# A perceiver block on one core: the last 65 context rows of each batch, taken as one half-length section per four batches

## The chip, the cores and the metric

The kernel runs on one core of one Trainium2 chip. Its time is the device time of one execution in microseconds (us); of a kernel that was run several times the median is given. The profile is taken from one further execution, which has a time of its own. The engines have short names here: PE is TensorE (PEld its weight loads), DVE is VectorE, ACT is ScalarE, POOL is GpSimd, SP is SyncE, which here issues DMAs. A name with a q (SPq) is the instruction queue of that engine.

## The reference, cut to what matters

Everything is float32. Eight batches of 64 rows of 512 numbers go through three blocks with residual sums: a cross attention to a context of 1601 rows per batch, a causal attention among the 64 rows, and a mixture of eight experts with two shared ones. The change lies in the cross attention:

```python
k = key_value @ Wk.T + bk          # key_value: (8, 1601, 512), Wk: (512, 512)
v = key_value @ Wv.T + bv
scores = einsum('bhqd,bhkd->bhqk', q, k) / sqrt(32)      # 16 heads of 32
s = where(scores >= 0, scores + 1, 1 / (1 - scores))
attn = s / sum(s, -1)
context = einsum('bhqk,bhkd->bhqd', attn, v)             # then @ Wo.T + bo
```

So 8 x 1601 context rows are multiplied by two 512 x 512 matrices, and each product is used by one batch.

## The kernel before, in words

**Sections and products of halves.** The 1601 rows of a batch are three sections of 512 rows and a rest of 65 (`TAIL`), of which the 64 that begin the rest are called `ROUND`. For a section the product with a weight matrix is not taken as eight products of half-size blocks but as seven, by sums and differences of blocks (Strassen's scheme in Winograd's form). `weight_parts` (L323) forms four sums of blocks of a weight matrix on DVE, `right_parts` and `context_part` (L334, L341) four differences of blocks of the section on POOL, `multiply` (L353) one of the seven products on PE, and `products` (L365) hands out the seven as units: each is copied out of PSUM by ACT, joined by DVE, and in one case added on POOL. The list `ORDER` says which bank of PSUM each product adds to: the units 0, 2, 4, 6 share bank A, 3 and 5 share B, 1 has C. `products(i, True)` gives the keys of section i, `products(i, False)` its values. The seven units of a whole section and one matrix take `7 * PROD` of planned time, with `PROD = FULL / 2 = 1.715`.

**The rest of a batch.** `load_tail(b)` (L472), `tail_keys(b)` (L482) and `tail_values(b)` (L502) treat the 65 last rows of two batches, b and b + 1, together, and without products of halves: 16 matmuls of 130 columns for the keys, 4 of 512 columns for the values. They are called for b = 0, 2, 4, 6. The value of the very last row (row 1600) of all batches is formed once at the start by `plain_values(odd_x, odd_v, B)` (L444), and a small DMA that POOL issues puts it under the other 64 values of its batch (L512).

**The plan.** `Plan` holds units of PE work with planned lengths, `plan.add`, and other work that is due at a planned time, `plan.at`. `emit` writes all of it out in the order of these times. Attention is spread evenly over it: `step = (end - 14.0) / len(tiles_in)` is the planned time of a tile of 128 context rows, with `end` the planned end of all sections; `lag` sets the first tile behind the sections that it needs. A unit of attention (two tiles, or the one rest of a batch) has `score` on PE (four PSUM banks), four times `convert` (three ACT instructions, a reciprocal on DVE of 128x512 and an addition and sums on POOL), and `weigh` on PE (L622). Within an engine, the compiler's scheduler takes the instructions that it thinks ready, in the order of the text; after `act.bind()`, at the end of the first section's part, ACT keeps the order of the text exactly.

**Memory.** PSUM has 7 banks of the pool `ps_a` and one for the output of attention. In SBUF the pool `w8` has 14 buffers of 8 KB per partition: `wk`, `wv` and their sums (`sk`, `sv`) stay in four of them, the others go round among a section's rows (`cx`), its differences (`tx`), keys, values and the weights of the later blocks. The pool `at` has 5 buffers for the converted scores, and `tl` holds what belongs to the rests.

**Before the first section.** SP loads the first section, then the four tiles of x (`res`), the rests of batches 0 and 1 (`cxt`), and the second section; the ACT queue loads `wk`, `wv`, `wq`. PE multiplies section 0 with `wk` chunk by chunk as both arrive (`first_keys`, four PSUM banks that ACT copies out), then come `plain_values`, `tail_keys(0)`, `tail_values(0)`, the four layer norms of x (`first_rows`), the first two units of the values of section 0, the queries, and the rest of these values. The sums `sq` of `wq` are formed at the very start; `sv` and `sk` during the queries, by `sums_of_weights`.

Of the kernel before, what the change touches and what calls it, by code (L numbers as in the profile page):

```python
# [18 lines left out]
P = 128  # L19
# [18 lines left out]
SEC = 512  # L38
# [57 lines left out]
def perceiver_kernel(  # L96
# [78 lines left out]


# [21 lines left out]
    bk_t = bias_cols(bk, NC, "bk_t")  # L198
    wv = load_w(wvT, "wv", nc.scalar)
# [72 lines left out]
    class Norm:  # L272
# [11 lines left out]
        def factors(self):  # L284
            self.rs = lnp.tile([P, 1], F32, name="ln_rs")
            act.activation(self.rs, self.mv[:, 1:2], AF.Sqrt, bias=eps_t)
            nc.vector.reciprocal(self.rs, self.rs)
            self.nb = lnp.tile([P, 1], F32, name="ln_nb")
            nc.vector.scalar_tensor_tensor(
                self.nb, self.mv[:, 0:1], -1.0, self.rs, ALU.mult, ALU.mult  # L290
            )
# [31 lines left out]
    def weight_parts(w, name):  # L323
        parts = {"a11": w[:, 0:2, 0:256], "a12": w[:, 2:4, 0:256],
                 "a21": w[:, 0:2, 256:512], "a22": w[:, 2:4, 256:512]}
        t = w8(name).rearrange("p k (c f) -> p k c f", c=2)
        for k in range(4):
            parts[f"s{k + 1}"] = t[:, k]
        for d, a, b, op in (("s1", "a21", "a22", ALU.add), ("s2", "s1", "a11", ALU.subtract),
                            ("s3", "a11", "a21", ALU.subtract), ("s4", "a12", "s2", ALU.subtract)):  # L330
            nc.vector.tensor_tensor(parts[d], parts[a], parts[b], op)
        return parts

    def right_parts(x, n=SEC):  # L334
        return {"b11": x[:, 0:2, 0 : n // 2], "b12": x[:, 0:2, n // 2 : n],
                "b21": x[:, 2:4, 0 : n // 2], "b22": x[:, 2:4, n // 2 : n]}

    RIGHT = (("t1", "b12", "b11"), ("t2", "b22", "t1"), ("t3", "b22", "b12"), ("t4", "b21", "t2"))
    tparts = {}
# [25 lines left out]
    def products(i, keys, w=None, dst=None, scale=None, bias=bk_t):  # L365
# [27 lines left out]
        def unit(n):  # L393
            bank, a, b = ORDER[n]
            if n == 0:
                t = dst
                if t is None:
                    t = (kTs if keys else vs)[i] = w8("kT" if keys else "v")
                for f in range(2):
                    for r in range(2):  # L400
                        st[f, r] = t[:, 2 * f : 2 * f + 2, r * HF : (r + 1) * HF] if keys else \
                            t[:, 2 * r : 2 * r + 2, f * 256 : (f + 1) * 256]
            fresh = bank not in st
            if fresh:
                st[bank] = psa("ps_k" if keys else "ps_v").rearrange("p (k n) -> p k n", k=2)
            ps = st[bank]
            multiply(ps, w[a], tparts[i][b], keys, first=fresh)
            if n == 0:
                copy(st[0, 0], ps, 0)
            elif n == 1:  # L410
                join(st[0, 0], ps)
            elif n == 2:
                copy(st[0, 1], ps, 0)
            elif n == 3:
                copy(st[1, 1], ps, None)
            elif n == 4:
                u3 = snp.tile([P, 2, 256], F32, tag="sn", name="u3")
                copy(u3, ps, 1)
                nc.gpsimd.tensor_add(st[1, 1], st[1, 1], u3)
            elif n == 5:  # L420
                join(st[0, 1], ps)
            else:
                copy(st[1, 0], ps, 1)
# [26 lines left out]

    tails = {}

    ROUND = TAIL - 1


    odd_x = const.tile([P, NC, B], F32, name="odd_x")
    for c in range(NC):
        nc.gpsimd.dma_start(
            out=odd_x[:, c, :],
            in_=ctxT[:, c * P : (c + 1) * P, SKV - 1 : SKV].rearrange("b p s -> p (b s)"),  # L460
        )
    odd_v = const.tile([B, E], F32, name="odd_v")
# [7 lines left out]


    def load_tail(b):  # L472

        cx = tails[b, "x"] = tlp.tile([P, NC, 2 * TAIL], F32, name="cxt", bufs=1)
        for k in range(2):
            nc.sync.dma_start(
                out=cx[:, :, k * ROUND : (k + 1) * ROUND],
                in_=ctxT[b + k, :, NSEC * SEC : SKV - 1].rearrange("(c p) s -> p c s", p=P),
            )
        nc.gpsimd.tensor_copy(cx[:, :, 2 * ROUND :], odd_x[:, :, b : b + 2])  # L480

    def tail_keys(b):  # L482
        kT = tlp.tile([P, NG, 2, TAIL], F32, name="kTt")
        cx = tails[b, "x"]
        for g in range(NG):
            ps = psa("ps_kt")[:, : 2 * TAIL]
            for c in range(NC):
                nc.tensor.matmul(  # L488
                    ps, wk[:, c, g * P : (g + 1) * P], cx[:, c, :], start=c == 0, stop=c == NC - 1
                )  # L490
            for s in (slice(0, ROUND), slice(ROUND, TAIL)):
                act.activation(
                    kT[:, g, :, s],
                    ps[:, 2 * s.start : 2 * s.stop].rearrange("p (k s) -> p k s", k=2),
                    AF.Identity, bias=bk_t[:, g : g + 1],
                )
        for k in range(2):
            tails[b + k, "k"] = kT[:, :, k, :]

    def tail_values(b):  # L502
        x = tails[b, "x"]
        ps = psa("ps_vt")
        for c in range(NC):
            nc.tensor.matmul(  # L506
                ps, x[:, c, 0 : 2 * ROUND], wv[:, c, :], start=c == 0, stop=c == NC - 1
            )
        for k in range(2):
            v = tails[b + k, "v"] = tlp.tile([P, E], F32, name="vt")  # L510
            act.copy(v[:ROUND], ps[k * ROUND : (k + 1) * ROUND])
            nc.gpsimd.dma_start(out=v[ROUND:TAIL, :], in_=odd_v[b + k : b + k + 1, :])  # L512
# [11 lines left out]
    def first_rows(tt):  # L524
# [4 lines left out]
        norm.stats()  # L529
# [535 lines left out]
    for i, (b, k) in enumerate(secs):  # L1065
        if i == 0:
# [3 lines left out]
            plan.at(0.05, lambda: (load_tail(0), weigh_bq(), wqp.update(weight_parts(wq, "sq"))))  # L1070
            plan.add(FULL, lambda: plain_values(odd_x, odd_v, B))
            plan.add(FULL, lambda: tail_keys(0))
            plan.add(FULL, lambda: tail_values(0))
            for tt in range(NTT):
                plan.add(0.5, lambda tt=tt: first_rows(tt))
            for n in range(4):
                plan.at(plan.now + 0.01 * n, lambda n=n: context_part("q", n))
            def sums_of_weights(to, w, name):

                with tc.issue_after(products.join.ins):  # L1080
                    to.update(weight_parts(w, name))

            plan.at(plan.now + 3.5 * PROD, lambda: sums_of_weights(wvp, wv, "sv"))
            plan.at(plan.now + 7.5 * PROD, lambda: sums_of_weights(wkp, wk, "sk"))
            wvp.update({"a11": wv[:, 0:2, 0:256], "a12": wv[:, 2:4, 0:256]})
# [32 lines left out]
        if k == NSEC - 1:  # L1118
            if b % 2 == 0 and b:
                plan.at(plan.now - 20.0, lambda b=b: load_tail(b))  # L1120
                plan.add(FULL, lambda b=b: tail_keys(b))
                plan.add(FULL, lambda b=b: tail_values(b))
# [22 lines left out]
    for u, time in enumerate(when):  # L1145
# [4 lines left out]
        if u == 3 * nu:  # L1150
            plan.at(time, clear)
    for tt in range(NTT):
# [578 lines left out]
```

## Time and profile before

| | us |
|---|---|
| median of 3 runs | 1362.18 (1360.87 to 1362.47) |
| the profiled execution | 1363.89 |
| its span, first to last instruction | 1362.3 |
| PE busy | 1349.4 (99%) |
| DVE busy | 977.8 (72%) |
| ACT busy | 676.2 (50%) |
| POOL busy | 765.1 (56%) |

A page of the profile gives the busy time of the engines, the span in 40 slices, the chain of work that ended last, and groups of equal instructions (count, busy time, mean time of one, idle time of the engine ahead of them and what ended it). Further views show the same trace in order of time, in stretches, or by tile. In the order-of-time view a row has the start, the time that the merged instructions took together, engine, line of the kernel, operation, output and inputs, shape and count. Each float32 matmul leaves two records, so a count of 8 is four matmuls. A record's own time holds the time that it needs to run through the array; what a record costs PE in a stream is the distance to the next start. The context is sent to SBUF with its rows as columns, so "128x130" is 130 context rows.

### The profile page before, as it was taken

Reading aid. Unit: us, or ns where it says so; the run is one execution under the profiler, and the core shown is the slowest. Engines: PE = TensorE matmul, PEld = TensorE weight load, DVE = VectorE, ACT = ScalarE, POOL = GpSimd, SP = SyncE. Lnnn points to the kernel's source line nnn. Section 1 sums busy time; section 2 is a strip of 40 time slices with the busy share of each in tenths; the row PEclk is TensorE's granted clock in tenths of the full one; section 3 lists DMA queues with packets and bytes.
Section 4 is the critical chain, followed back from the end, with each engine's and each line's share of the span. In section 5 each row is a group of like instructions: output and inputs, shape, how many; then the busy total and the mean of one; then the engine's idle time right before and its main releaser. Section 6 shows DMA issues by size and latency. Waiting matters only on the chain.

```text
span 1362.3 us, 37675 instructions
## 1 busy us (share of the span) xinstructions
PE 1349.4 (99%) x16554; PEld 1118.1 (82%) x16554; DVE 977.8 (72%) x859; ACT 676.2 (50%) x1436; POOL 765.1 (56%) x682
## 2 busy tenths in 40 slices
PE   9999999999999999999999999999999999999997
PEld 6888888888788888878888877578898999977786
DVE  2899999997999997999998999876976300010314
ACT  3566666665766666666656667435322211122230
POOL 3999999887978887888878876710200000000020
PEclk9999999999999999999999999999999999999999
DMA  7111111122401131112122104256555937788731
GB/s 210 64 33 33 33 33 64 33 79 72 156 10 64 33 110 41 33 33 63 42 62 81 64 33 163 88 177 238 190 200 157 337 133 266 265 303 322 274 92 32
DMA packets 87212, 160.63 MB, mean 118 GB/s; under 512 B 13467, under 2 KB 15035, under 8 KB 87045
## 3 DMA queue, kind: packets, MB, share of 16 engines
q1 hardware_dynamic: 79988, 140.61, 30.5%
q0 software_dynamic: 4704, 13.91, 2.9%
q10 hardware_dynamic: 2352, 3.67, 0.9%
q8 instruction: 131, 2.15, 0.7%
q14 instruction: 37, 0.30, 0.1%
HBM read 147.44 MB, written 10.72 MB: 116 GB/s over the span
## 4 chain that ended last, share of the span: by engine, by line
PE 95%; DMA 2%; DVE 1%; ACT 1%; issue 0%; SPq 0%; DVEq 0%
PE ps_v L359 22%; PE ps_k L359 21%; PE ps_h L1564 9%; PE ps_hh L359 7%; PE ps_hr L359 7%; PE ps_s L572 6%; PE y L1476 4%; PE y L1485 4%; PE ps_o L622 4%; PE y L1052 2%; PE ps_h L1040 2%; PE ps_aq L729 1%; PE ps_kt L488 1%; PE ps_vt L506 1%; PE ps_ap L801 1%; PE ps_wo L679 1%
## 5 line engine op out<-in xcount | busy, mean ns | idle before, releaser
L590 DVE RECIPROCAL neg<-neg 128x512 f32<-128x512 f32 (+1 forms) x224 | 686.9, 3096 | 55.0 <-ACT neg L87 48.5
L591 POOL TENSOR_TENSOR at<-at,neg 128x512 f32<-128x512 f32 (+1 forms) x224 | 269.3, 1208 | 107.5 <-DVE neg L590 100.1
L603 POOL TENSOR_TENSOR tot<-tot,at 128x512 f32<-128x512 f32 (+1 forms) x176 | 223.7, 1271 | 13.3
L87 ACT ACTIVATE neg<-neg,one_t 128x512 f32<-128x512 f32 (+1 forms) x224 | 157.8, 705 | 0.0
L87 ACT ACTIVATE neg<-ps_s 128x512 f32<-128x512 f32 (+1 forms) x224 | 127.9, 571 | 55.4 <-PE ps_s L572 54.8
L1564 PEld LDWEIGHTS ps_h<-xgT,w1t 128*128 128x128 f32 x896 | 123.0, 191 | 27.8 <-issue 26.1
L1569 ACT ACTIVATE hT<-ps_h,b1e 128x128 f32<-128x128 f32 (+3 forms) x112 | 42.6, 380 | 194.9 <-PE ps_h L1564 194.9
L359 PE MATMUL ps_v<-sv,tx 128*128 128x256 f32 x576 | 134.3, 383 | 0.0
L1564 PE MATMUL ps_h<-xgT,w1t 128*128 128x128 f32 (+3 forms) x896 | 129.2, 287 | 0.0
L1467 POOL DMA_DIRECT2D ys_d<-yo x10 | 5.4, 541 | 219.6 <-DVE yo L1466 219.6
L87 ACT ACTIVATE at<-ps_s 128x512 f32<-128x512 f32 (+1 forms) x224 | 128.5, 574 | 0.0
L359 PE MATMUL ps_k<-tx,sk 128*128 128x256 f32 x552 | 128.4, 384 | 0.0
L359 PEld LDWEIGHTS ps_v<-sv,tx 128*128 128x128 f32 x576 | 107.2, 190 | 17.0 <-issue 1.9
L359 PEld LDWEIGHTS ps_k<-tx,sk 128*128 128x128 f32 x552 | 102.7, 190 | 16.0 <-ACT at L87 0.8
L87 ACT COPY v<-ps_v 128x512 f32<-128x512 f32 x96 | 56.4, 588 | 93.7 <-PE ps_v L359 93.6
L87 ACT ACTIVATE kT<-ps_k,bk_t 128x256 f32<-128x256 f32 (+1 forms) x142 | 60.3, 478 | 66.9 <-PE ps_k L359 66.9
L1458 DVE COPY xgT<-pt_x 128x512 f32<-128x512 f32 (+3 forms) x12 | 6.8, 593 | 119.4 <-PE pt_x L1457 119.4
L359 PE MATMUL ps_v<-wv,cx 128*128 128x256 f32 x384 | 89.7, 383 | 0.6 <-DVE kT L387 0.6
L359 PE MATMUL ps_k<-cx,wk 128*128 128x256 f32 x368 | 86.2, 384 | 2.0 <-ACT at L87 1.3
L572 PEld LDWEIGHTS ps_s<-qT,kT 32*64 32x64 f32 x6144 | 70.3, 130 | 17.0 <-issue 14.5
L359 PEld LDWEIGHTS ps_v<-wv,cx 128*128 128x128 f32 x384 | 71.6, 190 | 12.3 <-DVE kT L387 1.5
L359 PEld LDWEIGHTS ps_k<-cx,wk 128*128 128x128 f32 x368 | 68.6, 190 | 12.3 <-ACT at L87 1.5
(286 smaller groups left out, 2258.8 us busy)
## 6 DMA issues: line engine op xcount, KB each, us to landing
w1t<-in_W_dram SPq DMA_DIRECT2D x32, 1024.0 KB, 10.4
w2t<-in_W_dram SPq DMA_DIRECT2D x32, 1024.0 KB, 9.7
cx<-in_ctxT_dram SPq DMA_DIRECT2D x23, 1024.0 KB, 5.2
w1t<-in_sW_dram SPq DMA_DIRECT2D x14, 1024.0 KB, 6.5
w2t<-in_sW_dram SPq DMA_DIRECT2D x14, 1024.0 KB, 6.0
wo<-in_woT_dram SPq DMA_DIRECT2D x4, 1024.0 KB, 5.5
awq<-in_aWq_dram SPq DMA_DIRECT2D x4, 1024.0 KB, 5.6
awp<-in_aWp_dram SPq DMA_DIRECT2D x4, 1024.0 KB, 5.6
```

The source lines that it names most:

```text
L87: ins = getattr(self.engine, name)(*args, **kw)
L359: nc.tensor.matmul(ps[:, k, :], l[:, c, k * P : (k + 1) * P], r[:, c, :], start=first and k == 0 and c == 0, stop=last and c == 1, skip_gr ...
L572: nc.tensor.matmul(ps[j][h, k, g, :], kT[rows, g, h], qT[rows, g, b * SQ : (b + 1) * SQ], start=True, stop=True, skip_group_check=True,)
L590: nc.vector.reciprocal(neg, neg)
L591: nc.gpsimd.tensor_add(pos, pos, neg)
L603: nc.gpsimd.tensor_add(tot, tot, at[:, :, i])
L622: nc.tensor.matmul(accs[b][32 * j : 32 * j + 32, g, :], v[:w, (4 * g + j) * 32 : (4 * g + j + 1) * 32], at[j // 2][:w, j % 2, k, g, :], st ...
L1040: nc.tensor.matmul(ps[:, :N0], w0[0, q][:, c, r * P : (r + 1) * P], shared_x["x"][:, c, :N0], start=c == 0, stop=c == NC - 1,)
L1476: nc.tensor.matmul(self.y[k], hT[:, s : s + w], w2t, start=first, stop=last)
L1485: nc.tensor.matmul(y[d // 2][:, d % 2, :], w2t[:, d * P : (d + 1) * P], hT[:, : self.n], start=first and d % 2 == 0, stop=last, skip_group ...
L1564: nc.tensor.matmul(ph[:, : blk.n], w1t[:, c, f : f + P], blk.x[:, c, :], start=c == 0, stop=c == NC - 1,)
L1569: nc.scalar.activation(hT[:, : blk.n], ph[:, : blk.n], AF.Gelu, bias=blk.bias(hc))
```

## The change

The rests of four batches, without their last rows, are 4 x 64 = 256 rows: half the length of a section. They are now loaded together (`load_tails`, for h = 0 and h = 1), into a `w8` buffer whose other half takes the four differences (`tail_parts`, POOL), and multiplied as seven products of halves with the same block sums of the weights (`tail_products`), keys and values. `products` has gained a half length `hf`. The first four batches are done at the start, the other four after the last section of batch 4. The values go to a DRAM tile `vt_d`, from which SP reads 65 rows for each batch (`load_vt`). The last rows of all batches are padded to 32 columns and multiplied with `wk` and `wv` in four strips of 32 output partitions (`odd_rows`); four transposes turn their keys. The sums `sk` and `sv` are now formed at the very start, the layer norms' statistics are put behind them on DVE, and `sq` behind the layer norms. The loads of the first rests stand ahead of those of x on SP.

```diff
+    ROUND = TAIL - 1
+    NQB = B // 2
+
+    def load_tails(h):
+        t = w8("cxt")
+        cxs["t", h] = t[:, :, 0:256]
+        for k in range(NQB):
+            nc.sync.dma_start(
+                out=t[:, :, k * ROUND : (k + 1) * ROUND],
+                in_=ctxT[h * NQB + k, :, NSEC * SEC : SKV - 1].rearrange("(c p) s -> p c s", p=P),
+            )
+        tparts["t", h] = right_parts(t, 256) | {
+            f"t{n + 1}": t[:, n, 256:512].rearrange("p (c s) -> p c s", c=2) for n in range(4)
+        }
...
     bk_t = bias_cols(bk, NC, "bk_t")
+    tparts = {}
+    load_tails(0)
     wv = load_w(wvT, "wv", nc.scalar)
...
-    def products(i, keys, w=None, dst=None, scale=None, bias=bk_t):
+    def products(i, keys, w=None, dst=None, scale=None, bias=bk_t, hf=HF, fit=lambda ps: ps):
...
-                st[bank] = psa("ps_k" if keys else "ps_v").rearrange("p (k n) -> p k n", k=2)
+                st[bank] = psa("ps_k" if keys else "ps_v")[:, : 2 * hf].rearrange(
+                    "p (k n) -> p k n", n=hf if keys else 256
+                )
             ps = st[bank]
             multiply(ps, w[a], tparts[i][b], keys, first=fresh)
+            ps = fit(ps)
...
-    odd_v = const.tile([B, E], F32, name="odd_v")
+    odd_k = const.tile([P, NG, B], F32, name="odd_k")
+    vt_d = dram.tile([B, TAIL, E], F32, name="vt_d")
...
-    def load_tail(b):
-    def tail_keys(b):
-    def tail_values(b):
...
+    def odd_rows():
+        ps = psa("ps_odd")
+        for c in range(NC):
+            for j in range(4):
+                w = (wk, wv)[j // 2]
+                nc.tensor.matmul(
+                    ps[32 * j : 32 * j + 32, 0:256], odd_x[:, c, :],
+                    w[:, c, (j % 2) * 256 : (j % 2 + 1) * 256],
+                    start=c == 0, stop=c == NC - 1, skip_group_check=True,
+                )
+        rows = [np2("odd") for _ in range(2)]
+        for j in range(4):
+            act.copy(
+                rows[j // 2][0:B, (j % 2) * 256 : (j % 2 + 1) * 256], ps[32 * j : 32 * j + B, 0:256]
+            )
+        nc.scalar.dma_start(
+            out=vt_d[:, ROUND:TAIL, :].rearrange("b o e -> b (o e)"), in_=rows[1][0:B, :]
+        )
+        pt = psa("pt_odd")[:, : NG * B].rearrange("p (g b) -> p g b", g=NG)
         for g in range(NG):
+            nc.tensor.transpose(pt[:, g, :], rows[0][0:B, g * P : (g + 1) * P], ident[0:B, 0:B])
+        for g in range(NG):
+            act.activation(odd_k[:, g, :], pt[:, g, :], AF.Identity, bias=bk_t[:, g : g + 1])
+
+    def tail_parts(h):
+        p = tparts["t", h]
+        for d, a, b in RIGHT:
+            nc.gpsimd.tensor_tensor(p[d], p[a], p[b], ALU.subtract)
+
+    def tail_products(h):
...
+        def values():
+            v = tails["v", h] = at4("vh").rearrange("p (k e) -> p k e", k=2)
+            return v
+        ku = products(
+            ("t", h), True, dst=keys, hf=P,
+            fit=lambda ps: ps.rearrange("p k (b s) -> p k b s", s=ROUND),
+        )
+        vu = products(("t", h), False, dst=values, hf=P)
...
+            for k in range(NQB):
+                nc.sync.dma_start(
+                    out=vt_d[h * NQB + k, 0:ROUND, :],
+                    in_=v[(k % 2) * ROUND : (k % 2 + 1) * ROUND, k // 2, :],
                 )
+        return ku[:2] + vu[:2] + ku[2:] + vu[2:-1] + [last]
+
+    def load_vt(b):
+        tails[b, "v"] = tlp.tile([P, E], F32, name="vt")
+        nc.sync.dma_start(out=tails[b, "v"][0:TAIL, :], in_=vt_d[b])
...
-            plan.at(0.05, lambda: (load_tail(0), weigh_bq(), wqp.update(weight_parts(wq, "sq"))))
-            plan.add(FULL, lambda: plain_values(odd_x, odd_v, B))
-            plan.add(FULL, lambda: tail_keys(0))
-            plan.add(FULL, lambda: tail_values(0))
+            def early():
+                tail_parts(0)
+                wkp.update(weight_parts(wk, "sk"))
+                wvp.update(weight_parts(wv, "sv"))
+                early.done = weight_parts.last
+                weigh_bq()
+            def sums_q():
+                with tc.issue_after(Norm.last.ins):
+                    wqp.update(weight_parts(wq, "sq"))
+            plan.at(0.05, early)
+            plan.add(2.0, odd_rows)
+            for u in tail_products(0):
+                plan.add(PROD / 2, u)
             for tt in range(NTT):
-                plan.add(0.5, lambda tt=tt: first_rows(tt))
+                plan.add(0.5, lambda tt=tt: first_rows(tt, early.done))
+            plan.at(plan.now, sums_q)
...
-            plan.at(plan.now + 3.5 * PROD, lambda: sums_of_weights(wvp, wv, "sv"))
-            plan.at(plan.now + 7.5 * PROD, lambda: sums_of_weights(wkp, wk, "sk"))
...
-            if b % 2 == 0 and b:
-                plan.at(plan.now - 20.0, lambda b=b: load_tail(b))
-                plan.add(FULL, lambda b=b: tail_keys(b))
-                plan.add(FULL, lambda b=b: tail_values(b))
+            if b == NQB:
+                plan.at(plan.now - 30.0, lambda: load_tails(1))
+                plan.at(plan.now - 15.0, lambda: tail_parts(1))
+                for u in tail_products(1):
+                    plan.add(PROD / 2, u)
...
+        if units[u][1] == nu - 1:
+            plan.at(time, lambda b=units[u][0]: load_vt(b))
```

In `first_rows` the statistics now carry `tc.issue_after(behind.ins)`: an order on DVE, not a wait for data.

## The prediction

> **What bounds the kernel now.** I read the page first: the busy time of the engines, then the chain of work that ended last.
>
> ```profile
> PE 1349.4 (99%) x16554; PEld 1118.1 (82%) x16554; DVE 977.8 (72%) x859; ACT 676.2 (50%) x1436; POOL 765.1 (56%) x682
> PE 95%; DMA 2%; DVE 1%; ACT 1%; issue 0%; SPq 0%; DVEq 0%
> ```
>
> PE is busy from end to end and is nearly the whole chain; so the change is worth what it takes from PE's stream, less the time in which it makes PE wait. Second, the view in order of time, PE alone, at the two kinds of place where rests are done: the start, and (from the view of all engines) the rest of batches 4 and 5.
>
> ```profile
> 19.99 3.59 PE L447 MATMUL ps_v<-wv,odd_x 128*8 128x512 f32 x8
> 23.99 3.82 PE L488 MATMUL ps_kt<-cxt,wk 128*128 128x130 f32 x32 [0.41 <-DMA cxt<-in_ctxT_dram]
> 27.64 3.60 PE L506 MATMUL ps_vt<-wv,cxt 128*128 128x512 f32 x8
> 31.08 1.91 PE L302 MATMUL pt<-ident,xn 128*128 128x128 f32 x16
> ```
>
> ```profile
> 519.24 3.85 PE L488 MATMUL ps_kt<-cxt,wk 128*128 128x130 f32 x32
> 522.92 3.60 PE L506 MATMUL ps_vt<-wv,cxt 128*128 128x512 f32 x8
> 526.45 3.95 PE L729 MATMUL ps_aq<-xnT_a,awq 128*64 128x64 f32 x128
> ```
>
> Look at the starts: 11.09 us from 19.99 to 31.08, and 7.21 us from 519.24 to 526.45. The other two rests read the same way: 3.67 + 3.63 us at 308 to 319, 3.68 + 3.64 us at 728 to 738.
>
> **Removed from PE.** 11.09 + 7.30 + 7.21 + 7.32 = 32.9 us, including 0.4 us of waiting for `cxt`.
>
> **Added to PE.** Three shapes, each with a row of this trace. Products of halves with 128 columns exist already in the shared expert; with 256 columns in every section; four strips of 32 outputs in the sums of attention:
>
> ```profile
> 896.31 3.73 PE L359 MATMUL ps_hh<-xnT,w1t 128*128 128x128 f32 x32
> 899.88 1.95 PE L359 MATMUL ps_hh<-xt,sw 128*128 128x128 f32 x16
> ```
>
> ```profile
> 99.22 1.89 PE L359 MATMUL ps_k<-cx,sk 128*128 128x256 f32 x8
> 100.94 1.89 PE L359 MATMUL ps_k<-tx,wk 128*128 128x256 f32 x8
> ```
>
> ```profile
> 153.69 0.64 PE L643 MATMUL ps_sum<-tot,ones 128*32 128x256 f32 x8
> 154.26 1.99 PE L359 MATMUL ps_k<-tx,sk 128*128 128x256 f32 x8
> ```
>
> 32 records of 128 columns pass in 3.57 us: 112 ns each. 8 records of 256 pass in 1.72 us: 215 ns each. 8 records in strips pass in 0.57 us: 71 ns each, a third of a full one, so the strips run side by side.
> - Keys, for each half of the batches: 7 products of 4 matmuls of 128 columns, 56 records x 112 ns = 6.3 us.
> - Values: 7 products of 2 matmuls of 256 columns, 28 records x 215 ns = 6.0 us. Together 12.3 us, twice: 24.6 us.
> - `odd_rows`: 16 matmuls of 256 columns in strips, 32 records x 71 ns = 2.3 us. Its four transposes, 8 records at no more than 112 ns: under 0.9 us, I take 0.6.
>
> Sum 27.5 us; balance 27.5 - 32.9 = -5.4 us. By place: the start gets 15.2 for 11.1 us (+4.1), the middle 12.3 for 21.8 (-9.5).
>
> [...]
>
> **What lies beside PE.**
> - DVE: eight sums of weights move from 40 to 53 us to about 10 to 22 us, where DVE waits for x (its statistics at 14.60, 16.88, 18.69 and 20.16 us each follow a wait for `res`). The first reciprocal of attention (53.44 us) waits for ACT, not for these sums; moving them gains nothing there. Added: 8 joins of 256 columns, at 422 ns in the shared expert's rows, 3.4 us in all.
> - ACT: removed 32 + 8 + 1 copies, 15 us (5.8 + 4.0 + 4.6 + 0.6); added 28 at about 0.37 (10.4) and 8 small ones (2.5). Even.
> - POOL: removed 8 DMA issues and 4 copies (4.1 + 0.8 us); added 8 differences and 4 additions of half the size of the 1.27 us rows, 8 us. 56% busy; hidden.
> - SP: the loads of `cxt` are 8 as before, but four now stand ahead of x. A pair takes SP 0.92 to 1.22 us, so x is asked for some 2 us later, behind 0.5 MB that come in pieces of 256 bytes; a pair landed 2.8 us after its issue when alone. I put x 3 to 5 us later, at 18 to 25 us. Cover: PE has the tail products, 15 us, ahead of the transposes of x. The 16 transfers by way of `vt_d` are small, and a rest's `weigh` comes 20 us after its `score` (136.1 and 156.2 us).
> - Slots: the second `cxt` holds one `w8` buffer from about 481 to 531 us. SP got buffers at 481.5 (section 15), 498.2 and 503.0 (weights); shifted by one, section 15 lands at 503.4, and POOL used it at 507.8. It fits, by 4 us.
> - `end` in the plan falls from 622.8 to 618.0, `step` from 5.85 to 5.81 (0.8% denser attention), and attention starts 3.7 planned us later.
>
> **New waits, which the trace does not show.** At the start `odd_rows` must be copied out by ACT before the transposes can run, and PSUM is tight: 7 banks, four with section 0's keys. What ACT does there:
>
> ```profile
> 21.14 1.52 ACT L87 ACTIVATE xn<-res,ln_nb,ln_rs 128x512 f32<-128x512 f32 x2 [3.02 <-DVE ln_nb L289]
> 22.57 0.46 ACT L87 ACTIVATE ln_rs<-ln_mv,eps_t 128x1 f32<-128x1 f32 x2
> 23.27 1.52 ACT L87 ACTIVATE xn<-res,ln_nb,ln_rs 128x512 f32<-128x512 f32 x2 [0.24 <-DVE ln_nb L289]
> 24.70 2.39 ACT L87 ACTIVATE kT<-ps_k,bk_t 128x512 f32<-128x512 f32 x4
> ```
>
> The keys of section 0 are finished on PE at 19.9, but ACT empties their banks only from 24.70, because the layer norms stand ahead of them in its order and wait for x. If that order stays while x comes 4 us later, the banks come free at about 29; PE then has `odd_rows` and one product (to 23.1) and stands for 6 us. If the layer norms, now behind the weights' sums on DVE, fall behind the copies on ACT too, the cost is two copies (0.37 each) and the hand-overs: about 1. Between 0 and 6 I take 1.7, near the lower end: the same crowded stretch cost PE only 0.41 us before, and the norms are pushed back by the change.
> In the middle, a half-length unit lasts 0.86 us and shares its bank with the unit two places on, while ACT may have a `convert` in between (0.6 + 0.6 + 0.74 us). Bounds: 0 (the rows at 896 us run such units without a gap) and 4 converts x 1.5 = 6. I take 0.5.
>
> Forecast: -5.4 + 1.7 + 0.5 = -3.2 us: 1360.7 on the profiled execution's 1363.89, which lies 1.7 above the median; from the median, **1359.0**.
>
> **Rivals.**
> 1. *The start pays all back.* ACT keeps its order and PE stands 6 us near 23 us: -5.4 + 6 + 0.5 = +1.1, 1363.3. For it: the ACT rows above. Against: the new order behind the weights' sums.
> 2. *Attention sets the pace (slower).* DVE is close to full wherever attention runs; the stretches of 50 us:
>
> ```profile
> 50.00:100.00 50.00, 50.00 (x830) 43.09 (x829) 49.58 (x22) 34.05 (x67) 45.70 (x37) 1.00 0.17 55
> 200.00:250.00 50.00, 50.00 (x811) 42.62 (x800) 48.26 (x23) 32.04 (x68) 46.80 (x40) 1.00 0.14 45
> 300.00:350.00 50.00, 50.00 (x891) 41.97 (x891) 40.62 (x21) 32.25 (x71) 39.78 (x34) 1.00 0.17 50
> ```
>
> Columns are length, PE, PEld, DVE, ACT, POOL, clock, DMA. DVE has 48.26 of 50; 0.8% more makes 48.6. If that is already too much (the point is where DVE's idle 1.4 us per 50 are hand-overs that can't shrink), PE waits in `weigh`, the shorter middle buys nothing, and the later start of attention (+4) is the whole result: 1366. Against: 300 to 350 us, where DVE falls to 40.62 and can catch up.
> 3. *The strips don't overlap with real weights*: `odd_rows` 32 x 215 ns = 6.9 instead of 2.3, +4.6: 1363.6. The row at 153.69 speaks against it.
> 4. *A slot comes too late* near 500 us: section 15 lands after 516 instead of 503, POOL's four differences (5 us) push its third product: up to 6 us, 1365. The spare 20 us between POOL's work and PE's use speak against it.
>
> **How the numbers follow.** About 0.2% (2.7 us) is what a measurement of this kernel can tell from no change: faster means under 1359.5, slower above 1364.9. Forecast 0.56, of which 0.48 under 1359.5 and 0.08 above, own range 1355.5 to 1361; rival 1: 0.20 (0.03 faster, 0.12 same, 0.05 slower); rival 2: 0.14, slower; rival 3: 0.03, same; rival 4: 0.07 (0.01 faster, 0.02 same, 0.04 slower). Faster 0.52, same 0.25, slower 0.23. Low end: no new wait (-5.4) and the 1.3 us that PE once waits for ACT near 664 us gone: 1355.5. High end: rival 2, 1366.
>
> **What would show it.** Right: 14 units of 0.86 us at each of two places, `odd_rows` within 2.5 us, the first transposes of x near 36 us, nothing of `ps_kt` and `ps_vt`, PE's idle time as before. Wrong: a gap of PE between 22 and 30 us ended by ACT (rival 1), `weigh` waiting for POOL (2), 200 ns between records of `ps_odd` (3), a gap before the keys of section 15 ended by POOL or a DMA (4).

## The result, and the profile after

| | kernel before | changed kernel |
|---|---|---|
| median of the runs (lowest to highest), us | 1361.81 (1360.23 to 1362.51, 6 runs) | 1365.65 (1364.32 to 1367.47, 6 runs) |
| ratio after/before, 95% interval | | 1.0029 (1.0020 to 1.0039) |
| the profiled execution, us; its span | 1363.89; 1362.3 | 1365.34; 1363.7 |
| mean granted clock of that execution | 0.999 | 0.996 |

The change costs 3.8 us (0.3%); a gain of 3.2 was forecast. The two profiled executions lie only 1.45 us apart, because that of before was 2.1 us above its median and that of the changed kernel 0.3 under. I use their rows for places and durations, and the medians for the balance.

The page of the changed kernel, engines and chain:

```profile
PE 1346.8 (99%) x16590; PEld 1123.1 (82%) x16590; DVE 971.8 (71%) x868; ACT 676.0 (50%) x1432; POOL 764.7 (56%) x684
PE 95%; ACT 1%; DVE 1%; issue 1%; POOL 1%; DMA 0%; ACTq 0%; DVEq 0%; POOLq 0%
```

PE is busy 2.6 us less, although the kernel is slower. In the chain DMA's 2% are gone, and issue and POOL have come in with 1% each. The waits of PE, longest sums first (total, times, longest):

```profile
PE ps_k L376 <- issue: 2.3, 1, 2.3
PE ps_s L626 <- DVE kTt L405: 2.3, 1, 2.3
PE ps_o L676 <- POOL at L645: 1.5, 2, 1.0
```

"issue" stands for a wait that no semaphore of the trace ended. All three are new, and all lie behind the start: near 734, 516 and 884 us. The rows of PE at the first and the third:

```profile
733.07 0.92 PE L376 MATMUL ps_k<-cx,wk 128*128 128x256 f32 x3
...
736.29 2.97 PE L376 MATMUL ps_k<-cx,wk 128*128 128x256 f32 x13 [2.31 <-issue]
```

```profile
882.19 1.10 PE L676 MATMUL ps_o<-at,v 128*32 128x64 f32 x64
...
884.35 0.30 PE L676 MATMUL ps_o<-at,vt 65*32 65x64 f32 x2 [0.95 <-POOL at L645]
885.21 0.71 PE L676 MATMUL ps_o<-at,vt 65*32 65x64 f32 x25 [0.56 <-POOL at L645]
```

In the kernel before, a product of the shared expert stood between the last two weighings, and PE did not wait there:

```profile
880.23 1.10 PE L622 MATMUL ps_o<-at,v 128*32 128x64 f32 x64
881.26 2.84 PE L1052 MATMUL y<-w2t,hTq 128*128 128x512 f32 x6
884.03 0.65 PE L622 MATMUL ps_o<-at,vt 65*32 65x64 f32 x32
```

Summed over the trace between PE's first and last record, PE's idle time is 8.86 us, after 4.70 before.

**The start went as forecast.** PE alone in order of time:

```profile
18.95 0.41 PE L507 MATMUL ps_odd<-wk,odd_x 128*32 128x256 f32 x2
...
20.50 0.39 PE L507 MATMUL ps_odd<-wv,odd_x 128*32 128x256 f32 x2
21.46 0.26 PE L522 MATMUL pt_odd<-ident,odd 8*128 8x8 f32 x2 [0.57 <-ACT odd L87]
...
28.51 2.05 PE L376 MATMUL ps_k<-cxt,sk 128*128 128x128 f32 x16 [0.89 <-ACT kTt L87]
...
35.61 1.58 PE L324 MATMUL pt<-ident,xn 128*128 128x128 f32 x13
```

The strips of `odd_rows` run side by side and are done in 1.93 us (18.95 to 20.88). The transposes of x begin at 35.61 us; they began at 31.08.

**The second place did not.** The same view around the tail of batches 4 to 7:

```profile
514.79 1.20 PE L626 MATMUL ps_s<-qT,kT 32*64 32x64 f32 x88
518.28 1.15 PE L626 MATMUL ps_s<-qT,kT 32*64 32x64 f32 x40 [2.29 <-DVE kTt L405]
519.36 1.26 PE L376 MATMUL ps_k<-cxt,sk 128*128 128x128 f32 x8
520.55 1.12 PE L770 MATMUL ps_akv<-xnT_a,awkv 128*64 128x64 f32 x16
```

A score stops after 88 of its 128 records and stands for 2.29 us. And after it everything is slow: 16 records of `ps_akv` take 1.12 us, while the same instruction took 0.69 at 308.94 us in this trace. What DVE was doing, from the view of all engines:

```profile
511.40 6.55 DVE L644 RECIPROCAL neg<-neg 128x512 f32<-128x512 f32 x2
...
517.87 0.36 DVE L405 TENSOR_TENSOR kTt<-ps_k,kTt 128x256 f32<-128x256 f32 x1
```

`tail_products` issues two units of the keys, then two of the values. These four hold four of the seven PSUM banks, and a score needs four. Two of the held ones come free only by a join on DVE, and the joins stand behind two reciprocals of attention, 6.55 us. That is the wait.

**The clock.** Stretches of 50 us; columns are start and end, length, PE, PEld, DVE, ACT, POOL (instructions in brackets), clock, DMA share, GB/s. The kernel before:

```profile
500.00:550.00 50.00, 50.00 (x924) 41.86 (x923) 41.98 (x20) 31.71 (x66) 40.53 (x35) 1.00 0.26 80
...
850.00:900.00 50.00, 49.72 (x527) 27.85 (x526) 44.25 (x34) 20.67 (x42) 27.69 (x23) 1.00 0.40 131
```

The changed kernel:

```profile
500.00:550.00 50.00, 47.71 (x862) 41.83 (x862) 38.59 (x21) 29.61 (x62) 37.37 (x31) 0.97 0.29 91
...
850.00:900.00 50.00, 48.40 (x512) 26.00 (x511) 42.80 (x33) 17.68 (x39) 28.19 (x23) 0.97 0.38 126
```

The granted clock in this trace is 1.0 from 4.88 to 520.29 us, 0.5 for 3.41 us, 1.0 to 885.52, 0.5 for 3.41 us again, then 1.0 up to the end of the work. The trace of before has no stretch at half clock ahead of its last 6 us. Both new stretches begin just after waits of PE, 2.0 us behind the one near 516 us and 0.3 us behind those near 884; each can cost, by an estimate from its length, up to 3.41 x 0.5 = 1.7 us on top of the wait. (Together they cost 2.7 us: PE's last record ends at 1356.96 us, less 8.86 idle that is 1348.10 us of work, against 1345.43 for the same records without half clock in experiment 2.)

### The profile page after: what moved, and what is told of

It reads as the page before. It is cut to its first block, busy times and chain, and to the rows that moved or that the text cites. A ratio compares the mean times of both kernels' runs of the same rounds, so it can differ in the third digit from the quotient of the medians.

```text
span 1363.7 us, 37808 instructions
## 1 busy us (share of the span) xinstructions
PE 1346.8 (99%) x16590; PEld 1123.1 (82%) x16590; DVE 971.8 (71%) x868; ACT 676.0 (50%) x1432; POOL 764.7 (56%) x684
## 3 DMA queue, kind: packets, MB, share of 16 engines
q8 instruction: 132, 2.16, 0.6%
## 4 chain that ended last, share of the span: by engine, by line
PE 95%; ACT 1%; DVE 1%; issue 1%; POOL 1%; DMA 0%; ACTq 0%; DVEq 0%; POOLq 0%
PE ps_v L376 23%; PE ps_k L376 23%; PE ps_h L1626 9%; PE ps_hh L376 7%; PE ps_hr L376 6%; PE ps_s L626 6%; PE y L1538 4%; PE y L1547 4%; PE ps_o L676 4%; PE ps_h L1094 1%; PE ps_aq L783 1%; PE ps_k L465 1%; PE ps_ap L855 1%; PE ps_wo L733 1%; DVE neg L644 1%
## 5 line engine op out<-in xcount | busy, mean ns | idle before, releaser
L626 PE MATMUL ps_s<-qT,kT 32*64 32x64 f32 x6144 | 77.3, 231 | 2.3 <-DVE kTt L405 2.3
```

The source lines that it names most:

```text
L626: nc.tensor.matmul(ps[j][h, k, g, :], kT[rows, g, h], qT[rows, g, b * SQ : (b + 1) * SQ], start=True, stop=True, skip_group_check=True,)
```

## The experiments

Theory A: PE's work shrank by about what was forecast, and three waits (for DVE near 516, for nothing visible near 734, for POOL near 884 us) and half clock after them took more than that. Theory B: attention, with DVE at its head, sets the pace, and a wait that is removed comes back elsewhere.

The kernel before measured 1362.5 us on the chip of the first four experiments, 1366.3 and 1366.1 on a second chip (experiments 5 to 11) and 1365.5 on a third (experiment 12), so each kernel is compared within its own group. All edits are against the changed kernel unless a base is named; kernel 2 is the kernel of experiment 2, and so on.

**1. The changed kernel again.**

> The changed kernel itself, a second trace. Theory A (its lost time sits in three places: PE's gaps near 516 and 734 us and from 883 to 888 us, and the stretches of 3.41 us at half clock that followed the first and the third): the gaps of about 2.3 us near 516 (ended by DVE's join of kTt) and about 2 us from 883 (ended by POOL) come back, as they follow from the order of the work; the half-clock stretches come back after some of them; the gap near 734 us may differ in length, as an instruction fetch between two loads of 1 MB decides it. 1364 to 1367 us. Theory B (attention on DVE sets the pace, the gaps are only where that shows): the same time, but the gaps lie elsewhere.

Measured: 1365.87 (1363.64 to 1369.48, 10 runs), ratio to before 1.0025 (1.0015 to 1.0036). The same waits, and half clock for 3.41 us from 520.55 and from 885.77 us. Both traces of the kernel show them.

**2. Keys before values at the second place.**

```diff
-        return ku[:2] + vu[:2] + ku[2:] + vu[2:-1] + [last]
+        return (ku + vu[:-1] if h else ku[:2] + vu[:2] + ku[2:] + vu[2:-1]) + [last]
```

> Only for the second four batches, the seven units of the keys come first and then the seven of the values, instead of two and two in turn; the work is the same. Theory A: the gap near 516 us is a lack of PSUM banks (two banks of keys and two of values wait for joins that stand behind two reciprocals on DVE, 6.55 us); with the values later only two banks are held, the gap of 2.3 us goes and with it the half-clock stretch (1.7 us): 4.0 us less than the changed kernel, about 1361.6 us. Theory B: DVE has the same work, the wait moves to another place, 1365 us as before.

Measured: 1361.43 (1360.91 to 1363.42, 10 runs), ratio to before 0.9993 (0.9983 to 1.0002): 4.4 us under the changed kernel in the same group. The view of all engines:

```profile
514.26 1.95 PE L376 MATMUL ps_k<-cxt,sk 128*128 128x128 f32 x16
...
516.14 1.59 PE L626 MATMUL ps_s<-qT,kT 32*64 32x64 f32 x128
...
519.15 0.36 DVE L405 TENSOR_TENSOR kTt<-ps_k,kTt 128x256 f32<-128x256 f32 x1
...
519.57 0.69 PE L770 MATMUL ps_akv<-xnT_a,awkv 128*64 128x64 f32 x16 [0.75 <-DVE kTt L405]
```

DVE's join is as late as ever (519.15, behind the same two reciprocals), but the score finds four free banks and runs through; 0.75 us of waiting remain. Theory A holds, B falls. The same trace settles the sum of PE's work, since it has no half clock ahead of the end: its last PE record ends at 1352.61 us with 7.18 idle, that of before at 1355.41 with 4.70. Work: 1345.43 against 1350.71, 5.28 us less (5.1 against the second trace of before, experiment 5); forecast was 5.4.

**3. The last weighing and all that is timed by it later.**

```diff
-    weighed[-1] = when[-1] + 11.0
+    weighed[-1] = when[-1] + 14.0
```

> The last product of attention with the values is due 3 planned us later, so that the shared expert's matmuls come ahead of it on PE. Theory A: PE no longer stands for POOL near 883 us (1.9 us) and no half-clock stretch follows (1.7 us): up to 3.6 us less than the changed kernel, about 1362 us; the last chain starts 3 us later but has other work beside it. Theory B: the end of attention moves back by 3 us and all behind it: 1366 to 1368 us.

Measured: 1371.28 (1370.48 to 1375.23, 4 runs), 5.4 us over the changed kernel: a miss for both theories. The view of all engines, of the longest of the four executions:

```profile
891.38 0.64 PE L697 MATMUL ps_sum<-tot,ones 128*32 128x256 f32 x8
...
892.50 1.75 DVE L704 RECIPROCAL rec<-rec 128x256 f32<-128x256 f32 x1 [0.31 <-ACT rec L87]
...
897.08 1.27 PE L376 MATMUL ps_hh<-xt,sw 128*128 128x128 f32 x7 [3.52 <-DVE sw L353]
```

The waits for POOL are gone, but the edit moved the sums too, and with them the loads and weight sums of the next products, which are ordered behind the sums' reciprocal on DVE. PE then waited 3.52 us for `sw`.

**4. Both edits.**

> Both edits together. Theory A: the sum, 7 to 8 us less than the changed kernel, about 1358 us, under the kernel before; no half-clock stretch but that at the very end. Theory B: 1365 us or more.

Measured: 1368.06 (1366.84 to 1369.0, 5 runs), ratio to before 1.0036 (1.0022 to 1.0050). The first edit still takes 3.2 us off the second; the wait of 3.52 us for `sw` stays. The second edit was wrong in what it moved, so it could not judge the wait for POOL.

**5. The kernel before again** (second chip from here on).

> The kernel before, unchanged, once more under the profiler. Its first profiled execution (1363.89) lay 1.7 above its median, so the two profiles understate the loss. Theory A (that execution was merely long by scatter): the same six waits of PE, 4.7 us in all, no stretch at half clock ahead of the last 6 us, and a time of 1361 to 1363. Theory B (before has stretches at half clock in some executions too): one or more stretches of 3.41 us at 0.5, and a time above 1363.5.

Measured: 1362.59. PE's idle time is 3.44 us (4.70 in the first trace; the wait near 664 us is 0.46 instead of 1.34, and that near 775 is gone); no half clock ahead of the end. Theory A for this run. But it lies 3.7 us under the median of its own chip, so it does not show what a usual execution there does. Of the 25 timed runs of before beside it, six had a mean clock of 0.997 and took 1368.5 us in the mean, thirteen had 0.999 and took 1365.1: half clock seems to come to the kernel before too, in some executions (theory B). No trace of one was taken.

**6. The load of awp later, on kernel 2.** The line `st["wp"] = load_w(aWp, "awp")` moves from the end of `queries` to the end of `exps`.

> On the kernel with keys before values, one more edit: the load of the second projection's weights (awp) is issued after the exponentials instead of after the queries, so that it no longer stands beside the load of a section near 730 us. Theory A (the 1.9 to 2.3 us without a releaser near 733 us are a fetch of instructions held up behind two loads of 1 MB): that gap shrinks to under 1 us, the time falls by 1.5 to 2 to about 1359.6. Theory B (the fetch costs that much wherever it falls, whatever else is loading): the gap stays or only moves, time unchanged at 1361.4.

Measured: 1363.88 (1363.37 to 1365.89, 10 runs), ratio to before 0.9985 (0.9973 to 0.9997). Now only `cx` is loading there, and the wait near 733 us is still 1.65 us, as it is 1.57 in experiment 7, which leaves the load where it was. So the load of awp is not the cause. The load of `cx` is not cleared by this; experiment 12 comes back to it.

**7. Only the last weighing and its sums later, on kernel 2.** `last unit` stands for a test of the unit's number.

```diff
-        plan.at(weighed[u], lambda u=u: weigh(*units[u]))
+        plan.at(weighed[u] + 0.8 * (last unit), lambda u=u: weigh(*units[u]))
-            plan.at(min(when[last] + 2.4 * step, done), lambda b=b: sums(b))
+            plan.at(min(when[last] + 2.4 * step, done) + 0.8 * (last unit), lambda b=b: sums(b))
```

> On the kernel with keys before values, one other edit: the last weighing and its sums are placed 0.8 planned us later, and nothing else is moved, so that a product of the shared expert stands between them and the weighing ahead of them. Theory A (PE's three waits for POOL near 881 to 884 us, 1.95 us in all, come from the last weighing being placed before POOL is done): they go, time about 1359.6. Theory B (what hangs on the sums, the loads of the shared expert's weights and the sums of them on DVE, comes later by as much and PE waits there instead, as when weighing and chain were both moved by 3): a wait of 1.5 us or more between 886 and 900 us, time 1361.4 or more.

Measured: 1362.73 (1361.51 to 1365.9, 10 runs), ratio to before 0.9974 (0.9964 to 0.9984). PE alone in order of time:

```profile
878.69 2.84 PE L1106 MATMUL y<-w2t,hTq 128*128 128x512 f32 x6
881.47 0.65 PE L676 MATMUL ps_o<-at,vt 65*32 65x64 f32 x32
881.94 0.78 PE L697 MATMUL ps_sum<-tot,ones 128*32 128x256 f32 x8
...
887.11 1.13 PE L733 MATMUL ps_wo<-wo,ctT 128*128 128x512 f32 x2 [1.63 <-POOL ctT L712]
```

The order that the kernel before has there is back: six records of `y`, 2.84 us, between the last two weighings. The waits for POOL are gone. Of the 1.95 us, 1.63 come back at 887 us, for POOL's `ctT` at the end of the chain from the sums. So theory B is right about the wait, and still the run was 1.2 us quicker than kernel 6 in the same group; experiment 10 bears on why.

**8. All three edits.**

> All three edits: keys before values at the second place, awp after the exponentials, the last weighing 0.8 later. Theory A (the predicted balance of PE was right and the three waits with their half-clock stretches took it): 4.2 + 1.8 + 1.9 under the changed kernel, about 1357.7, 4 us under the kernel before. Theory B (attention on DVE sets the pace, so that a wait removed comes back elsewhere): 1360 or more.

Measured: 1361.97 (1361.53 to 1362.85, 8 runs), ratio to before 0.9970 (0.9958 to 0.9982). 1.9 us under kernel 6, and level with kernel 7: moving awp is worth nothing. The change now wins 4.3 us on the kernel before on this chip: the 4 us of theory A, but without awp's share, and at the time that theory B gave.

**9. The changed kernel and kernel 2 on the second chip.**

> The changed kernel once more, beside the three that follow, on one chip, since chips differ by some microseconds. Theory A (three waits of PE and the half-clock stretches after them): 3 to 5 us over the kernel before, mean clock 0.995 to 0.997 in most executions. Theory B (the result hangs on the chip): no more than 1 us over the kernel before.

> Keys before values at the second place, as in the first run of this edit. Theory A: 4 us under the changed kernel on the same chip. Its profiled execution had no stretch at half clock ahead of the end, but eight of its ten timed ones showed a mean clock of 0.997 or 0.998; theory A says that the wait for POOL near 882 us is followed by half clock in some executions and not in others, by where the windows of 3.41 us fall: a profile with a phase other than 7.47 us (the first full-clock stretch's start) shows one.

Measured: the changed kernel 1369.55 (6 runs), ratio 1.0030 (1.0018 to 1.0042); kernel 2 1364.78 (12 runs), ratio 0.9989 (0.9980 to 0.9999): 4.8 us apart. The loss does not hang on the chip. The stretches of kernel 2, first its trace of experiment 2:

```profile
700.00:750.00 50.00, 48.08 (x897) 41.30 (x895) 40.95 (x19) 30.22 (x61) 38.67 (x31) 1.00 0.24 76
850.00:900.00 50.00, 47.96 (x538) 27.73 (x537) 43.47 (x41) 20.24 (x44) 27.01 (x23) 1.00 0.42 138
```

and the trace of the same program here:

```profile
700.00:750.00 50.00, 46.77 (x763) 39.96 (x762) 38.97 (x18) 29.27 (x59) 36.55 (x31) 0.97 0.24 75
850.00:900.00 50.00, 48.26 (x516) 26.04 (x515) 42.68 (x35) 17.56 (x38) 28.17 (x23) 0.97 0.40 132
```

One program, waits at the same two places, and half clock in one execution and not in the other, as theory A asked. A half-clock stretch lasts 3.413 us in these traces, and the lengths of the full-clock stretches between are multiples of it: 515.41 us is 151 of them and 361.81 is 106 (changed kernel), 730.45 is 214 (kernel 2 here). So the changes of clock seen here lie on a grid with that step. The grid lies differently in the two executions of kernel 2: the first full-clock stretch began at 7.47 us in experiment 2 and at 4.32 here. I laid each trace's grid over PE's rows and summed PE's idle time in the windows of 3.413 us between its marks:

| execution | window, us | PE idle in it, us | what PE runs around it | half clock next |
|---|---|---|---|---|
| changed kernel | 516.88 to 520.29 | 1.41 | score, 32x64 | yes |
| changed kernel | 882.10 to 885.52 | 1.52 | weighing, 65x64 | yes |
| changed kernel, run 9 | 516.41 to 519.82 | 2.29 | score | yes |
| changed kernel, run 9 | 881.63 to 885.05 | 1.09 | weighing | no |
| kernel 2, run 2 | 881.29 to 884.70 | 1.19 | weighing | no |
| kernel 2, run 9 | 881.54 to 884.96 | 1.51 | weighing | yes |
| kernel 2, run 2 | 731.10 to 734.51 | 1.92 | products 128x256 | no |
| kernel 2, run 9 | 731.36 to 734.77 | 2.65 | products 128x256 | yes |
| kernel 7 | 885.11 to 888.52 | 1.63 | products 128x512 | no |

Windows of other traces fit: amid the score or the weighing 1.29 (experiment 1), 1.38 (experiment 11) and 1.87 us (experiment 3) were followed by half clock; amid products 1.83 us was not, 2.07 and 2.79 were (all experiment 3). A score beside products of 64 columns, with 1.35 us (changed kernel, 731.92 to 735.33), was not. What sets the clock, these traces do not show.

**10. Kernel 7 on the same chip as kernel 2.**

> Keys before values, and the last weighing 0.8 planned us later. In its first trace the 1.95 us for POOL near 882 us are gone, but PE waits 1.63 us for ctT at 885.5. Theory C (the chain of sums, reciprocal, product and ctT sets the time there, so the wait only moved): same time as keys before values alone, within 0.7 us. Theory D (a wait amid full products is not followed by half clock, one amid the narrow products of weighing is): mean clock 0.999 where the other has 0.997, and 1 to 1.7 us less.

Measured: 1362.19 (1361.5 to 1366.17, 12 runs), ratio to before 0.9978 (0.9966 to 0.9989): 2.6 us under kernel 2, more than theory D's 1 to 1.7. The mean clock is 0.999 in eight of twelve runs (0.998 in four); kernel 2's is 0.998 or less in ten of twelve. The wait that replaced the waits for POOL lies between full products and is not followed by half clock. At the same mean clock of 0.998 the two lie close, 1364.7 us in the mean (four runs) against 1364.8 (eight); at 0.999, 1361.9 (eight) against 1363.2 (two). D holds in kind, and most of the difference goes with the clock; that the whole 2.6 us is the clock was not shown.

**11. Keys before values at the start too.**

```diff
-        return (ku + vu[:-1] if h else ku[:2] + vu[:2] + ku[2:] + vu[2:-1]) + [last]
+        return ku + vu[:-1] + [last]
```

The base is kernel 2.

> Keys before values at the start too. Theory E (the start waits for ACT's queue, norms among the copies, whatever the order of the products): within 0.7 us of the kernel with this edit at the second place alone. Theory F (the interleaving pays at the start, where it puts two units between the two that share a bank): waits of PE for ACT between 22 and 34 us of 1 us or more beyond the present 1.46, time 1 to 2 us more.

Measured: 1364.58 (1363.93 to 1365.83, 10 runs), 0.2 under kernel 2. The wait of 0.89 us at the start is 0.56. Theory E holds: there the order matters little. Why is not shown; in the changed kernel ACT has emptied the banks of section 0's keys (19.75 us) before the tail begins.

**12. The third chain's keys later, on kernel 7.** In the loop over the chain's steps:

```diff
-            plan.at(time, fn)
+            plan.at(time + X * (tt == 2 and fn.__name__ == "keys"), fn)
```

X is 1.8 (one product of a section goes ahead of them) or 3.5 (two).

> Keys before values and the last weighing later, once more, as the base for the two that follow. Both theories: PE stands 1.5 to 3.2 us without a releaser near 732 us, after a weighing, a score and the keys of the third chain.

> On that base: the third chain's keys (32 records of 64 columns) come one product of a section later, so that 1.9 us of long products stand between the score of 128 records and them. Nothing else moves. Theory G (PE runs out of instructions because 192 short records in a row use up what was fetched faster than the next 16 KB come): the stall near 732 us is gone or under 0.3 us, time 1.5 us less. Theory H (the fetch is late for a reason of its own, whatever stands before it): a stall of 1.5 us or more, at the same instruction count or moved, time unchanged.

> The same with two products, 3.7 us, between the score and the chain's keys. Theory G: no stall, as with one. Theory H: a stall as before.

Measured in one group: base 1362.18 (10 runs, ratio to before 0.9981), X = 1.8: 1361.37 (8 runs, 0.9972), X = 3.5: **1359.65** (1358.97 to 1360.24, 5 runs), ratio to before **0.9964** (0.9949 to 0.9978). PE in order of time, the base:

```profile
727.00 1.59 PE L626 MATMUL ps_s<-qT,kT 32*64 32x64 f32 x128
728.52 0.69 PE L770 MATMUL ps_akv<-xnT_a,awkv 128*64 128x64 f32 x16
...
732.38 2.75 PE L376 MATMUL ps_k<-cx,wk 128*128 128x256 f32 x12 [1.65 <-issue]
```

X = 1.8:

```profile
728.50 1.99 PE L376 MATMUL ps_k<-cx,wk 128*128 128x256 f32 x8
...
732.13 0.34 PE L770 MATMUL ps_akv<-awkv,xnT_a 128*64 128x64 f32 x4 [0.68 <-issue]
```

X = 3.5:

```profile
728.56 3.72 PE L376 MATMUL ps_k<-cx,wk 128*128 128x256 f32 x16
732.21 0.69 PE L770 MATMUL ps_akv<-xnT_a,awkv 128*64 128x64 f32 x16
```

The traces list packets of instructions on a DMA queue of their own (page of the changed kernel, packets and MB: `q8 instruction: 132, 2.16, 0.6%`, so 16 KB each); I call one a fetch. A fetch starts at 729.9 us in all three traces; where PE stood, it goes on at 732.1 to 732.4. With 160 short records right ahead (the expectation says 192) PE stands for 1.65 us; with one long product between, for 0.68; with two, PE doesn't stand. Theory G holds in kind: the length of the stop went with what PE runs ahead of it. That PE had used up its instructions is my reading of this; the rows show a wait that no semaphore ended. The theory's numbers for one product (under 0.3 us of standing, 1.5 us less) were missed, with 0.68 and 0.8.

In all fourteen traces of changed kernels in which PE stands here, it stands at one place in its stream, after 22,721 of PE's instructions in the trace, and goes on 2.3 to 3.1 us after the fetch began. In the changed kernel the 251 ahead of that place took 3.1 us (33,400 of PE's instructions and 132 fetches in that trace: by estimate 253 a fetch, if all of them are PE's). In the kernel before, the same score and keys stand in a row too, but a long product of the rest follows, one of those that the change takes out:

```profile
731.46 1.60 PE L572 MATMUL ps_s<-qT,kT 32*64 32x64 f32 x128
732.98 0.69 PE L716 MATMUL ps_akv<-xnT_a,awkv 128*64 128x64 f32 x16
...
734.06 3.70 PE L506 MATMUL ps_vt<-wv,cxt 128*128 128x512 f32 x8
```

A fetch began at 733.32 us there, and PE did not stand. Why the fetch begins so late is open, and here theory H has a point: it starts at 729.9 us whatever PE has run. A rival that no run tests is the load of `cx`, 1 MB: where it is the only load (experiment 6), its transfers start from 726.92 to 730.47 us, and the fetch starts at 730.47.

## Why the prediction was wrong, point by point

- **What bounds the kernel: right.** PE's stream, less the waits that the change brings. Rival 2, attention setting the pace, falls: its 1366 lies near the measured 1365.65 by chance, and its sign, a weighing that waits for POOL, came only at the last one (1.5 us). With DVE's work unchanged, edits of order alone took 4.4 and 2.5 us away (experiments 2 and 12).
- **PE's balance of -5.4: right.** 5.28 measured (experiment 2). The rows of the shared expert and of the sections gave the prices of the new shapes; strips cost 1.75 us for a forecast 2.3 (16 matmuls in 8 steps of 0.215 us). Rival 3 falls.
- **The start: right.** New waits of PE there 0.57 + 0.89 = 1.46 us for 1.7; the transposes of x 4.53 us later for 5.8. ACT emptied section 0's keys at 16.48 to 19.75 us, ahead of the norms, so rival 1 falls.
- **"In the middle ... I take 0.5": the step that failed first.** It looked for what a bank waits for on ACT, and held each unit against the unit two places on in the same stream. The bank that was missing was a score's, and what held it was a join on DVE behind two reciprocals of attention. The rows of before show such a queue on DVE near this place, three reciprocals ahead of a join:

```profile
508.36 9.76 DVE L590 RECIPROCAL neg<-neg 128x512 f32<-128x512 f32 x3
518.04 0.63 DVE L387 TENSOR_TENSOR v<-ps_v,v 128x512 f32<-128x512 f32 x1
```

In place of the 0.5 us the wait cost 2.29 us and, in all four traces of kernels that had it, half clock; taking it away was worth 4.4 and 4.8 us.
- **"`end` in the plan falls from 622.8 to 618.0": priced at nothing, wrongly.** All later steps are sorted into PE's stream by due time. With the shorter middle the last weighing came ahead of the product that covered POOL (1.5 to 1.95 us; experiment 7 restores the order, but 1.63 us of waiting come back elsewhere).
- **The products taken out were counted as work alone.** Near 734 us PE went on into `ps_vt` during a fetch and did not stand; without `ps_vt` PE stood 1.5 to 3.2 us, and two long products ahead of the place took that away (experiment 12). "PE's idle time as before", among the signs that the forecast named, was thus the assumption that no later place changes.
- **The clock: not thought of.** The forecast let a wait cost its own length.
- **Balance.** Work -5.3; idle time 8.9 for 3.4 to 4.7, +4.2 to +5.4; two stretches at half clock, +2.7: +1.6 to +2.8 for +3.8 measured. The 1.0 to 2.2 us that are left stay open: no traced execution of before lies at the median of its chip.
- **The outcome slower was given 0.23**, mainly by rival 2, with the right sign and the wrong cause. Rival 4 fell: nothing waited for a slot near 500 us.

## What to carry to other kernels

When new PE units come between old ones in a hand-ordered stream, count the PSUM banks that are held at each score or other taker of several, and ask on which engine's queue each release stands, with the durations ahead of it. A shorter section moves the due time of all that follows: compare the order of the instructions behind the change, not only around it, and ask what a long product that goes away was hiding. A change of this kind is worth judging after its waits are gone: three edits of order turned +0.3% (first and second chip) into -0.36% (third chip), each against the kernel before beside it.

## What the runs showed of the hardware

- In these traces the changes of the granted clock lie on a grid of 3.413 us, which lies differently in different executions (first full-clock stretch from 7.47 and from 4.32 us, kernel 2). A window of it at full clock with 1.29 to 2.29 us of idle PE amid the narrow matmuls of score and weighing was followed by a window at half clock, one with 1.19 or 1.09 was not, nor one with 1.35 after a score and products of 64 columns; amid full products up to 1.92 was not, 2.07 and more was. Half clock came after a single gap of 2.29 us (changed kernel, experiment 9) and after 0.95 and 0.56 us in one window (changed kernel). So the waits for POOL near 882 us came without half clock in one execution of kernel 2, where the window held 1.19 us of idle PE, and with it in the other, where it held 1.51; that costs up to 1.7 us more, by estimate from half of the 3.41 us.
- PE stood 1.5 to 3.2 us, with no semaphore to end it, after a score of 128 short records followed by 32 more, and went on 2.3 to 3.1 us after a fetch of 16 KB of instructions had begun. One product between them (8 records of 256 columns, 1.99 us) left 0.68 us of it, two (16 records, 3.72 us) left none. In the trace with 3.23 us (kernel 2, experiment 9) the fetch began at 730.92 us, 1.0 later than with 1.65 us (experiment 12's base), and its transfer took 1.78 us for 0.97; why is open.
- Four strips of 32 outputs ran fully side by side with real weights: in the changed kernel four records start within 0.02 us of each other, and the next four 0.215 us later, so four matmuls of 256 columns take 0.43 us, as long as one alone.
